# Four graph layers on one core: a kept order of the vector, scalar and GpSimd work of mixing and layer 1, some of it asked for a number of passes later

## Chip, cores and metric

The kernel runs on one core of a Trainium2 chip. The metric is the device time in microseconds (us) of one execution. The kernel before was run three times; their median is the number that the change is measured against. Besides, one execution was recorded by the profiler, and every duration in this text is from that one.

## What is computed

The input `x` has 8 batches of 2048 nodes with 64 features, and all four layers use the same 2048 x 2048 0/1 adjacency matrix. Each layer is a residual with a layer norm:

```
x = layernorm(x + L0(x, H, adj))   # hypergraph attention, mixed with adj/deg @ (x W_ind)
x = layernorm(x + L1(x, adj))      # dinv * (adj + I) * dinv @ x @ W^T
x = layernorm(x + L2(x, emb, adj)) # Chebyshev supports, softmax support, node-wise weights
x = layernorm(x + L3(x, adj))      # three rounds of relu(v W1v + adj v W1e) W2
```

Only the end of layer 0 and layer 1 matter here. In layer 0 two vectors of every node are mixed: `industry` (adj/deg @ x W_ind) and `g` (the attention). Each gets a score `tanh(f @ fcW + fcb) @ av`, a softmax over the two scores gives the weights, and the weighted sum is added to `x` and normalized. Layer 1 scales that by `dinv`, multiplies it with the adjacency, then with a 64 x 64 matrix, scales by `dinv` again, adds the residual and normalizes.

## The kernel before

**Tiling.** Two batches of 64 features fill 128 partitions, so the 8 batches are 4 *pairs* (p). The 2048 nodes are 4 *chunks* (c) of 512. `(p, c)` is one tile of 128 x 512 numbers, and there are 16 of them. The adjacency lies in SBUF the whole time. A product with it is split into a high and a low part (`split`, L165: `hi` is a rounded copy by ScalarE at L170, `lo` the rest by VectorE or GpSimd at L171), so one product of one pair is 2 halves (g) x 16 node tiles x 2 parts x 2 chunks = 128 matmuls of 128x512. One such matmul is called a *pass* in this text.

**The stage.** Mixing and layer 1 run interwoven. A Python generator, `filler`, gives out passes one at a time: first the rest of the products of layer 0 (`ug` in the profile), then `layer1(p)` for the four pairs (`u`). `fill(n)` asks for n passes. The loop over the *steps* i = 0..15 (one step is one tile of mixing) places the mixing's own TensorE work between them: `mix_scores(i)`, passes, `mix_end(i-1)`, passes, `mix_ind(i+1)` and `mix_g(i+1)`, passes, `mix_weigh(i)`, passes; 8 passes at each place, 9 from step 5 on. For one tile this is

- `mix_ind`: matmul `pi`, then VectorE `ind = pi * inv` (L823);
- `mix_g`: loads `gn` and `r` (a tile of x), four transposes `pg`, ScalarE `gt` (L838), GpSimd `r += gn` (L839);
- `mix_scores`: four matmuls `pf`, four ScalarE tanh (L851), two VectorE differences `t` (L853), GpSimd `ind -= gt` (L855);
- `mix_weigh`: matmuls `pd`, ScalarE `th` (L864), VectorE `ind *= th` (L865);
- `mix_end`: four transposes `pt`, VectorE `r += pt` (L873), then `layernorm`: VectorE mean (L142) and centring (L143), ScalarE square (L148), VectorE variance (L150, L152), GpSimd power (L154), VectorE scaling (L157), store of `r` to `x1_hbm` (L879).

`l1_parts` loads a stored tile back (`y`, L894), GpSimd scales it (L895), and `split` makes the two parts `v0h`..`v3l` that layer 1's passes read. At the end of each half of a pair ScalarE copies the two accumulators out (`ut`, L948); `l1_end` then runs on each: four matmuls `po`, a load of the residual `x1` (L903), VectorE `r = po * dinv` (L905), GpSimd `r += x1` (L906), and a layernorm without centring, whose result is stored to `x2_hbm` (L911).

**Buffers.** All small matmuls share four PSUM buffers (tag `mm`); `r` of the mixing, `gn`, `ut0`, `inv0`, the staged loads (`y`, `x1`, tag `x`) and `ut` have two buffers each, the parts `v0h`..`v3l` one each. So `r` of step i+1 is loaded into the buffer of step i-1, after the store of that one.

**What sets the order.** Each engine takes its instructions strictly in the order of its queue. The matmuls and transposes are kept in program order (`tc.keep_in_program_order`, L175 and L178). Nearly all other work of this stage is not: a scheduler in the framework places it in the queues of VectorE, ScalarE, GpSimd and SyncE (which issues the loads and stores) by its own estimate of when each would be ready. `later(n, f)` (L296) puts a piece of program off until n passes have gone by; `tick()` counts, once at each pass. Before, it is used for the last step of each layernorm (7 passes after the rest, through `put_off`) and for `l1_end` (6 and 14 passes after the half).

After the mixing, `mix_scope` closes, its memory becomes `xn`, the normalized x of all pairs. The embedding is loaded into parts of it (L1009), `load_xn` fetches the finished pairs back from `x2_hbm` on ScalarE's queue (L923), and `make_el` builds layer 2's factors (`pb`, `el`, `bias`) while the passes of the last pair run. Then come `s`, `pt` and `ua` of layer 2's softmax support.

Of the kernel before, what the change touches and what calls it, by code (L numbers as in the profile page):

```python
# [30 lines left out]
F32 = mybir.dt.float32  # L31
# [25 lines left out]
def tile_gnn_fast(  # L57
# [72 lines left out]
            s = slice(b * F, (b + 1) * F)  # L130
            nc.vector.tensor_scalar(t[s, s], t[s, s], mean[s], None, op0=ALU.subtract)

    def layernorm(pool, r, dst, groups=2 * JT, centred=False, small=None, tag="ln_c", bufs=1, put_off=None):


        xc = pool.tile([P, groups, F], F32, tag=tag, name="ln_c", bufs=bufs)
        pool = small or pool
        if centred:
            squares, xc = xc, r
        else:  # L140
            mean = pool.tile([P, groups], F32, tag="ln_m", name="ln_m", bufs=2)
            nc.vector.tensor_reduce(mean, r, AX.X, ALU.add)  # L142
            nc.vector.scalar_tensor_tensor(  # L143
                xc, mean[:, :, None].to_broadcast([P, groups, F]), -1.0 / F, r,
                op0=ALU.mult, op1=ALU.add,
            )
            squares = r
        nc.scalar.activation(squares, xc, AF.Square)  # L148
        var = pool.tile([P, groups], F32, tag="ln_v", name="ln_v", bufs=2)
        nc.vector.tensor_reduce(var, squares, AX.X, ALU.add)  # L150
        vare = pool.tile([P, groups], F32, tag="ln_e", name="ln_e", bufs=2)
        nc.vector.tensor_scalar(vare, var, 1.0 / F, EPS, op0=ALU.mult, op1=ALU.add)  # L152
        rstd = pool.tile([P, groups], F32, tag="ln_r", name="ln_r", bufs=2)
        nc.gpsimd.tensor_tensor(rstd, vare, neg_half[:, :groups], ALU.pow)  # L154

        def end():
            nc.vector.tensor_tensor(dst, xc, rstd[:, :, None].to_broadcast([P, groups, F]), ALU.mult)  # L157

        (put_off or (lambda f: f()))(end)

    def grouped(a):

        return a.rearrange("p t (b f) -> p (t b) f", f=F)
# [132 lines left out]
    def later(n, f):  # L296

        pending.append([n, f])

    def tick():  # L300
        for e in pending:
            e[0] -= 1
        while pending and pending[0][0] <= 0:
            pending.pop(0)[1]()

    places = {}
    xc, part = {}, {}
# [88 lines left out]
    def fill(n):  # L396
        for _ in range(n):
            if next(filler, None) == "wait":
                break

    def first_parts(c, where):
        where.add(c)
# [8 lines left out]
    with tc.tile_pool(name="pa_ps", bufs=1, space=PSUM) as pps:  # L411
# [42 lines left out]
        make_upper_triangular(nc, tri_e, 1.0, diag=True)  # L454


        def after(what):
            tc.keep_in_program_order(nc.gpsimd.tensor_copy(seen_x, what))

        for t in range(5):  # L460
            if t in (0, 2):
                after(xt[1 + t][:, 0, 0:1])
            load_adj(t, 0)
        tc.keep_in_program_order(nc.gpsimd.dma_start(flat[:, 0:MIX], mixing))

# [105 lines left out]
        for t in range(NT):  # L571
# [39 lines left out]
                    start=t == 0, stop=t == NT - 1,  # L611
                )
            if t in paced:
                after(seen[:, t, 0, 0:1])
                load_adj(paced[t], 0)
            if t in (9, 11):
                parts(0, (t - 9) // 2)
# [187 lines left out]

    uts, invs, gts, inds, tts, rs = {}, {}, {}, {}, {}, {}
    xn, done, stored, due = [], [0] * NP, set(), set()
    steps = NP * NCH

    def mix_load(i):  # L810
# [7 lines left out]
    def mix_ind(i):  # L818

        pi = lps.tile([P, C], F32, tag="mm", name="pi", bufs=4)  # L820
        mm(pi, lhsT=bd_ind, rhs=uts.pop(i), start=True, stop=True)
        inds[i] = mp.tile([P, C], F32, tag="ind", name="ind", bufs=3)
        nc.vector.tensor_tensor(inds[i], pi, invs.pop(i), ALU.mult)  # L823

    def mix_g(i):

        p, c = divmod(i, NCH)
        gn = mp.tile([P, JT, P], F32, tag="gn", name="gn", bufs=2)
        nc.sync.dma_start(
            gn, gs_hbm.rearrange("(p t) f -> p t f", t=NT)[:, wide(c), p * P:(p + 1) * P]  # L830
        )
        rs[i] = mp.tile([P, JT, P], F32, tag="r", name="r", bufs=2)
        load_x(rs[i], p, c)
        pg = lps.tile([P, C], F32, tag="mm", name="pg", bufs=4)
        for j in range(JT):
            transpose(pg[:, cols(j, P)], gn[:, j, :])
        gts[i] = mp.tile([P, C], F32, tag="gt", name="gt", bufs=2)
        nc.scalar.activation(gts[i], pg, AF.Identity, bias=-1.0)  # L838
        nc.gpsimd.tensor_tensor(rs[i], rs[i], gn, ALU.add)  # L839

    def mix_scores(i):

        t1 = []
        for src in (inds[i], gts[i]):
            for b in range(2):

                s = slice(b * F, (b + 1) * F)
                pf = lps.tile([P, C], F32, tag="mm", name="pf", bufs=4)
                mm(pf, lhsT=fc2[s, :], rhs=src[s, :], start=True, stop=True)
                t1.append(mp.tile([P, C], F32, tag="t1", name="t1", bufs=4))  # L850
                nc.scalar.activation(t1[-1], pf, AF.Tanh, bias=fcb_col)  # L851
        for b in range(2):
            nc.vector.tensor_tensor(t1[b], t1[b], t1[2 + b], ALU.subtract)  # L853
        tts[i] = t1[0:2]
        nc.gpsimd.tensor_tensor(inds[i], inds[i], gts[i], ALU.subtract)  # L855

    def mix_weigh(i):

        pd = lps.tile([P, C], F32, tag="mm", name="pd", bufs=4)
        for b in range(2):  # L860

            mm(pd[b * F:(b + 1) * F, :], lhsT=av2, rhs=tts[i][b], start=True, stop=True)
        th = mp.tile([P, C], F32, tag="th", name="th", bufs=1)
        nc.scalar.activation(th, pd, AF.Tanh, scale=0.5)  # L864
        nc.vector.scalar_tensor_tensor(inds[i], th, 1.0, inds[i], op0=ALU.add, op1=ALU.mult)  # L865

    def mix_end(i):
        p, c = divmod(i, NCH)
        r = rs.pop(i)
        pt = lps.tile([P, C], F32, tag="mm", name="pt", bufs=4)  # L870
        for j in range(JT):
            transpose(pt[:, cols(j, P)], inds[i][:, cols(j, P)])
        nc.vector.scalar_tensor_tensor(  # L873
            r, pt.rearrange("p (t f) -> p t f", f=P), 0.5, r, op0=ALU.mult, op1=ALU.add
        )

        def end(f):
            f()
            nc.sync.dma_start(x1_hbm[p][:, wide(c), :], r)  # L879
            stored.add((p, c))  # L880
            if p == 0:
                first_parts(c, mixed)
            elif (p, c) in due:
                l1_parts(p, c)

        layernorm(mp, grouped(r), grouped(r), put_off=lambda f: later(7, lambda: end(f)))

    def l1_parts(p, c):

        if (p, c) not in stored:  # L890
            due.add((p, c))
            return
        y = staged("y")
        nc.sync.dma_start(y, x1_hbm[p][:, wide(c), :])  # L894
        nc.gpsimd.tensor_tensor(y, y, dinv[:, wide(c), None].to_broadcast([P, JT, P]), ALU.mult)  # L895
        part[p, c] = split(va, y, f"v{c}", 1, [P, JT, P])

    def l1_end(p, c, ut):
        po = lps.tile([P, JT, P], F32, tag="mm", name="po", bufs=4)
        for j in range(JT):  # L900
            mm(po[:, j, :], lhsT=ut[:, cols(j, P)], rhs=bd_w1, start=True, stop=True)
        x1 = staged("x1")
        nc.sync.dma_start(x1, x1_hbm[p][:, wide(c), :])  # L903
        r = lp.tile([P, JT, P], F32, tag="r", name="r", bufs=2)
        nc.vector.tensor_tensor(r, po, dinv[:, wide(c), None].to_broadcast([P, JT, P]), ALU.mult)  # L905
        nc.gpsimd.tensor_tensor(r, r, x1, ALU.add)  # L906

        def end(f):
            f()
            if p < NP - 1:  # L910
                nc.sync.dma_start(x2_hbm[p][:, wide(c), :], r)  # L911
            done[p] += 1
            load_xn()

        dst = xn[p][:, wide(c), :] if p == NP - 1 else r
        layernorm(lp, grouped(r), grouped(dst), centred=True, put_off=lambda f: later(7, lambda: end(f)))

    def load_xn():

        for p in range(NP - 1):  # L920
            if xn and done[p] == NCH:
                done[p] = 0
                nc.scalar.dma_start(xn[p], x2_hbm[p][:])  # L923

    def layer1(p):

        for g in range(2):
# [17 lines left out]
                    l1_parts(p + 1, t // JT)  # L945
            for k, c in enumerate(own):
                ut = va.tile([P, C], F32, tag="ut", name="ut", bufs=2)
                nc.scalar.copy(ut, u[c])  # L948
                later(6 + 8 * k, lambda p=p, c=c, ut=ut: l1_end(p, c, ut))

    def all_pairs():
        yield from remaining
# [59 lines left out]

    ets = [load_emb(c, xn[NP - 1][:, wide(c), :].rearrange("p t f -> p (t f)")) for c in range(NCH)]

    load_xn()

    def make_el(c):
        et = ets[c]
# [13 lines left out]
    for c in range(NCH):  # L1032
        make_el(c)
        fill(16)
    norms = staged("emb").rearrange("p t f -> p (t f)")[:, 0:NT * D].rearrange("p (t d) -> p t d", d=D)
    nc.sync.dma_start(norms, emb.rearrange("(t p) d -> p t d", p=P))
    nc.vector.tensor_tensor(norms, norms, norms, ALU.mult)
# [14 lines left out]
    def apt_tile(c, t):  # L1052
# [4 lines left out]
        nc.scalar.activation(pt, s, AF.Exp)  # L1057
        nc.vector.tensor_scalar(pt, pt, 1.0, None, op0=ALU.max)  # L1058
        if t == 0:
            accs[c] = lp.tile([P, C], F32, tag="r", name="acc", bufs=2)  # L1060
            nc.gpsimd.tensor_copy(accs[c], pt)
        else:
            nc.gpsimd.tensor_tensor(accs[c], accs[c], pt, ALU.add)  # L1063
# [1125 lines left out]
```

## Time and profile before

| | |
|---|---|
| three runs | 1975.02, 1979.12, 1979.89 us, median 1979.12 |
| the profiled execution | 1976.23 us; its span from first to last instruction 1974.4 us |
| TensorE matmul busy | 1870.6 us, 95% of the span |
| VectorE, ScalarE, GpSimd busy | 1001.6, 394.6, 530.7 us |
| mean granted TensorE clock | 0.980 |
| mixing's first `pi` to last `pt` | 229.8 to 494 us |
| layer 1's first pass to last pass | 315.8 to 556.6 us |

How to read it: a profile row of the timeline has the start, the duration, the engine, the line of the kernel, the operation with what it writes and reads, its shape and count, and in brackets how long the engine had sat idle before and what ended that. PE is TensorE, DVE VectorE, ACT ScalarE, POOL GpSimd; `SPq` rows are DMAs that SyncE issues, and their duration is that of the issue. A busy matmul engine is not one at its peak: ends of matmuls are modelled and overlap, so the distance from start to start counts.

### The profile page before, as it was taken

The numbers are of one execution on the slowest core, as the hardware profiler recorded it, in microseconds if no ns is written. First come the engines' busy times: TensorE is split into PE (matmuls) and PEld (weight loads), VectorE is DVE, ScalarE is ACT, GpSimd is POOL, SyncE is SP. The second block draws the span as 40 slices with busy tenths as digits, with TensorE's granted clock in tenths as the row PEclk, the third lists the DMA queues.
The fourth block names the chain that finished last, engine by engine and source line by source line (L and its number), as shares of the span: only waits on it lengthen the run. The fifth ranks groups of instructions, "written<-read, shape, count | busy, mean of one in ns | idle before, by whom it ended". The sixth has DMA issues, their size and how long they took to land.

```text
span 1974.4 us, 19582 instructions
## 1 busy us (share of the span) xinstructions
PE 1870.6 (95%) x7100; PEld 1214.4 (62%) x7100; DVE 1001.6 (51%) x1741; ACT 394.6 (20%) x771; POOL 530.7 (27%) x480
## 2 busy tenths in 40 slices
PE   6888899888799999999999999999999999999997
PEld 4666566555554444755565575556546787877875
DVE  7779555556432211347546736764786333343332
ACT  1455343333121121100000000000001222222211
POOL 3678654544254344301001100110001020100101
PEclk9999899899899999999999999999999999999998
DMA  9923334332400000301101110111101122121211
GB/s 310 314 88 106 125 123 145 125 115 71 155 17 27 0 27 22 119 30 49 64 35 43 55 50 27 48 62 35 43 32 34 38 55 52 46 56 48 54 27 24
DMA packets 94185, 143.10 MB, mean 72 GB/s; under 512 B 29232, under 2 KB 40112, under 8 KB 93696
## 3 DMA queue, kind: packets, MB, share of 16 engines
q1 hardware_dynamic: 83920, 105.39, 17.2%
q0 software_dynamic: 7760, 27.66, 4.2%
q10 hardware_dynamic: 2400, 8.72, 1.2%
q8 instruction: 58, 0.95, 0.2%
q14 instruction: 47, 0.39, 0.1%
HBM read 98.67 MB, written 43.06 MB: 72 GB/s over the span
## 4 chain that ended last, share of the span: by engine, by line
PE 76%; DVE 4%; DMA 4%; POOL 4%; issue 3%; ACT 1%; SPq 1%; POOLq 0%; DVEq 0%; ACTq 0%
PE u L175 32%; PE py L175 22%; PE ua L175 11%; PE ug L175 3%; PE pr L175 2%; POOL ln_r L154 2%; PE po L175 1%; PE pf L175 1%; PE pt L178 1%; PE s L175 1%; DMA x<-x_hbm 1%; POOL r L906 1%; DMA r<-in_x_n 1%; DMA x_hbm<-r 1%; PE pd L175 0%
## 5 line engine op out<-in xcount | busy, mean ns | idle before, releaser
L175 PE MATMUL py<-wp,xg 128*128 128x512 f32 x1024 | 475.2, 592 | 0.7 <-DMA xg<-u_hbm 0.7
L175 PEld LDWEIGHTS py<-wp,xg 128*128 128x128 f32 x1024 | 193.3, 189 | 161.4 <-issue 138.5
L1276 DVE TENSOR_TENSOR fcav<-py,emb_n 128x512 f32<-128x512 f32 x256 | 177.0, 691 | 134.9 <-PE py L175 129.1
L175 PE MATMUL ua<-pt,xn 128*128 128x512 f32 x512 | 230.2, 592 | 1.5 <-DVE pt L1058 1.5
L154 POOL TENSOR_TENSOR ln_r<-ln_e,neg_half 128x8 f32<-128x8 f32 x64 | 108.1, 1688 | 458.0 <-DVE ln_e L152 425.0
L1277 DVE TENSOR_REDUCE r<-fcav 128x32 f32<-128x512 f32 x256 | 175.6, 686 | 8.2
L175 PEld LDWEIGHTS ua<-pt,xn 128*128 128x128 f32 x512 | 96.9, 190 | 110.9 <-issue 104.0
L175 PE MATMUL u<-adj,v0h 128*128 128x512 f32 x384 | 148.7, 455 | 1.3 <-ACT h L1432 1.3
L175 PE MATMUL u<-adj,v0l 128*128 128x512 f32 x384 | 141.3, 436 | 0.0
L175 PE MATMUL u<-adj,v2l 128*128 128x512 f32 x384 | 139.9, 429 | 1.2 <-DVE v2l L171 1.2
L175 PE MATMUL u<-adj,v2h 128*128 128x512 f32 x384 | 141.0, 433 | 0.0
L175 PE MATMUL u<-adj,v1h 128*128 128x512 f32 x384 | 140.7, 433 | 0.0
L175 PE MATMUL u<-adj,v3l 128*128 128x512 f32 x384 | 138.7, 426 | 0.0
L175 PE MATMUL u<-adj,v1l 128*128 128x512 f32 x384 | 138.4, 427 | 0.0
L175 PE MATMUL u<-adj,v3h 128*128 128x512 f32 x384 | 138.3, 427 | 0.0
L1063 POOL TENSOR_TENSOR acc<-acc,pt 128x512 f32<-128x512 f32 x60 | 76.8, 1280 | 103.9 <-DVE pt L1058 103.2
L1058 DVE TENSOR_SCALAR pt<-pt 128x512 f32<-128x512 f32 x64 | 30.2, 472 | 146.5 <-ACT pt L1057 146.2
L1358 DVE SCALAR_TENSOR_TENSOR ar<-fcav,ar 128x512 f32<-128x512 f32 x64 | 45.4, 709 | 109.1 <-ACT ar L1357 109.1
L175 PEld LDWEIGHTS u<-adj,v0h 128*128 128x128 f32 x384 | 71.6, 191 | 37.3 <-issue 24.5
L175 PEld LDWEIGHTS u<-adj,v2l 128*128 128x128 f32 x384 | 72.4, 190 | 32.2 <-issue 16.4
L175 PEld LDWEIGHTS u<-adj,v1l 128*128 128x128 f32 x384 | 72.8, 190 | 29.2 <-issue 14.4
L175 PEld LDWEIGHTS u<-adj,v3l 128*128 128x128 f32 x384 | 72.0, 188 | 29.4 <-issue 14.9
(354 smaller groups left out, 2669.5 us busy)
## 6 DMA issues: line engine op xcount, KB each, us to landing
adj<-in_adj_t POOLq DMA_DIRECT2D x32, 512.0 KB, 7.5
fcav<-in_adj_t SPq DMA_DIRECT2D x64, 256.0 KB, 2.9
u_hbm<-ut SPq DMA_DIRECT2D x48, 256.0 KB, 2.9
xg<-u_hbm SPq DMA_DIRECT2D x96, 128.0 KB, 2.9
x_hbm<-r SPq DMA_DIRECT2D x28, 256.0 KB, 2.1
hs_hbm<-st ACTq DMA_DIRECT2D x8, 584.0 KB
xt<-in_x_t SPq DMA_DIRECT2D x16, 256.0 KB, 6.6
ut<-u_hbm SPq DMA_DIRECT2D x16, 256.0 KB, 3.1
```

The lines of the kernel that those rows point to most:

```text
L154: nc.gpsimd.tensor_tensor(rstd, vare, neg_half[:, :groups], ALU.pow)
L175: tc.keep_in_program_order(nc.tensor.matmul(*args, **kw))
L178: tc.keep_in_program_order(nc.tensor.transpose(dst, src, ident))
L906: nc.gpsimd.tensor_tensor(r, r, x1, ALU.add)
L1058: nc.vector.tensor_scalar(pt, pt, 1.0, None, op0=ALU.max)
L1063: nc.gpsimd.tensor_tensor(accs[c], accs[c], pt, ALU.add)
L1276: nc.vector.tensor_tensor(pr, py, e_b, ALU.mult)
L1277: nc.vector.tensor_reduce(r[:, j, b, cols(k, OH)], pr, AX.X, ALU.add)
L1358: nc.vector.scalar_tensor_tensor(ar.bitcast(F32), seen_a, 1.0, ar.bitcast(F32), op0=ALU.mult, op1=ALU.not_equal, accum_out=left[:, t, k:k ...
```

## The change

The order of nearly all VectorE, ScalarE and GpSimd work of mixing and layer 1 is now kept as the program has it (`pin` is `tc.keep_in_program_order`). A new helper, `after(n, f, ...)`, asks for a piece n passes from now, and for the next one some passes after that one; unlike `later`'s list, in which a piece waits for those ahead of it, each entry runs when its own count is over. The layernorm of the two places becomes `normalized`, which gives three pieces: `square`, 5 passes later `power`, 9 passes later `scale`. `l1_load` makes the load of the residual a piece of its own, at the end of the half. `load_xn` works only once `room` is set, after the second `make_el`. The first accumulator of layer 2 lies in another tile. `fill` now counts a pass that can't be given yet, and goes on, where it stopped before. The old local `after` of the first stage is only renamed.

The instructions are the same in kind and number, and so is the order on TensorE, but for the four groups of `pb`, which come 9 passes later. On the other four queues the orders differ from the mixing's first steps (VectorE) or fifth step (the others) on, up to the first tiles of layer 2's softmax support, and are the same before and behind.

```diff
-    def layernorm(pool, r, dst, groups=2 * JT, centred=False, small=None, tag="ln_c", bufs=1, put_off=None):
+    def layernorm(pool, r, dst, groups=2 * JT, centred=False, small=None, tag="ln_c", bufs=1):
...
+    soon = []
+    def after(n, f, *more):
+        soon.append([n, lambda: (f(), after(*more) if more else None)])
     def tick():
-        for e in pending:
+        for e in pending + soon:
             e[0] -= 1
         while pending and pending[0][0] <= 0:
             pending.pop(0)[1]()
+        for e in [e for e in soon if e[0] <= 0]:
+            soon.remove(e)
+            e[1]()
...
+    def normalized(pool, r, dst, centred, then):
...
+        def square():
+            if not centred:
+                pin(nc.vector.tensor_reduce(mean, r, AX.X, ALU.add))
+                pin(nc.vector.scalar_tensor_tensor(
+                    xc, mean[:, :, None].to_broadcast(wide_r), -1.0 / F, r, op0=ALU.mult, op1=ALU.add
+                ))
+            pin(nc.scalar.activation(squares, src, AF.Square))
+        def power():
+            pin(nc.vector.tensor_reduce(var, squares, AX.X, ALU.add))
+            pin(nc.vector.tensor_scalar(vare, var, 1.0 / F, EPS, op0=ALU.mult, op1=ALU.add))
+            pin(nc.gpsimd.tensor_tensor(rstd, vare, neg_half[:, :groups], ALU.pow))
+        def scale():
+            pin(nc.vector.tensor_tensor(dst, src, rstd[:, :, None].to_broadcast(wide_r), ALU.mult))
+            then()
+        return square, 5, power, 9, scale
...
      def mix_ind(i):
-        nc.vector.tensor_tensor(inds[i], pi, invs.pop(i), ALU.mult)
+        inv = invs.pop(i)
+        after(3, lambda: pin(nc.vector.tensor_tensor(inds[i], pi, inv, ALU.mult)))
      def mix_g(i):
-        nc.gpsimd.tensor_tensor(rs[i], rs[i], gn, ALU.add)
+        r = rs[i]
+        after(8, lambda: pin(nc.gpsimd.tensor_tensor(r, r, gn, ALU.add)))
      def mix_scores(i):
+        def differences():
+            for b in range(2):
+                pin(nc.vector.tensor_tensor(t1[b], t1[b], t1[2 + b], ALU.subtract))
+        pin(nc.gpsimd.tensor_tensor(inds[i], inds[i], gts[i], ALU.subtract))
+        after(5, differences)
      def mix_weigh(i):
+        after(4, lambda: pin(
+            nc.vector.scalar_tensor_tensor(inds[i], th, 1.0, inds[i], op0=ALU.add, op1=ALU.mult)
+        ))
      def mix_end(i):
-        layernorm(mp, grouped(r), grouped(r), put_off=lambda f: later(7, lambda: end(f)))
+        after(3, add_up, 0, *normalized(mp, r, r, False, end))
      def l1_parts(p, c):
+        def scale():
+            pin(nc.gpsimd.tensor_tensor(y, y, dinv[:, wide(c), None].to_broadcast([P, JT, P]), ALU.mult))
+        def cast():
+            part[p, c] = split(va, y, f"v{c}", 1, [P, JT, P], pin=True)
+        after(16, scale, 6, cast)
 -    def l1_end(p, c, ut):
+    def l1_end(p, c, ut, x1):
-        layernorm(lp, grouped(r), grouped(dst), centred=True, put_off=lambda f: later(7, lambda: end(f)))
+        after(4, add_up, 6, *normalized(lp, r, dst, True, end))
      def layer1(p):
...
-                nc.scalar.copy(ut, u[c])
-                later(6 + 8 * k, lambda p=p, c=c, ut=ut: l1_end(p, c, ut))
+                pin(nc.scalar.copy(ut, u[c]))
+                later(6 + 8 * k, lambda p=p, c=c, ut=ut, x1=l1_load(p, c): l1_end(p, c, ut, x1))
...
     for c in range(NCH):
         make_el(c)
         fill(16)
+        if c == 1:
+            room.append(True)
+            load_xn()
```

More of the change, by code (lines that the diff above doesn't have):

```diff
@@ L154, in layernorm @@
         nc.gpsimd.tensor_tensor(rstd, vare, neg_half[:, :groups], ALU.pow)
-        def end():
-            nc.vector.tensor_tensor(dst, xc, rstd[:, :, None].to_broadcast([P, groups, F]), ALU.mult)
-        (put_off or (lambda f: f()))(end)
+        nc.vector.tensor_tensor(dst, xc, rstd[:, :, None].to_broadcast([P, groups, F]), ALU.mult)
     def grouped(a):
@@ L398, in fill @@
             if next(filler, None) == "wait":
-                break
+                tick()
     def first_parts(c, where):
@@ L454, in tile_gnn_fast, with behind @@
         make_upper_triangular(nc, tri_e, 1.0, diag=True)
-        def after(what):
+        def behind(what):
             tc.keep_in_program_order(nc.gpsimd.tensor_copy(seen_x, what))
@@ L461, in tile_gnn_fast @@
             if t in (0, 2):
-                after(xt[1 + t][:, 0, 0:1])
+                behind(xt[1 + t][:, 0, 0:1])
             load_adj(t, 0)
@@ L613, in tile_gnn_fast @@
             if t in paced:
-                after(seen[:, t, 0, 0:1])
+                behind(seen[:, t, 0, 0:1])
                 load_adj(paced[t], 0)
@@ L807, in tile_gnn_fast @@
     xn, done, stored, due = [], [0] * NP, set(), set()
+    pin = tc.keep_in_program_order
+    def normalized(pool, r, dst, centred, then):
+        groups = 2 * JT
+        r, dst = grouped(r), grouped(dst)
+        wide_r = [P, groups, F]
+        var, vare, rstd, mean = (
+            pool.tile([P, groups], F32, tag=f"ln_{n}", name=f"ln_{n}", bufs=2) for n in "verm"
+        )
+        xc = pool.tile(wide_r, F32, tag="ln_c", name="ln_c", bufs=1)
+        squares, src = (xc, r) if centred else (r, xc)
+        def square():
[13 more added lines that the diff above has]
+        return square, 5, power, 9, scale
     steps = NP * NCH
@@ L837, in mix_g @@
         gts[i] = mp.tile([P, C], F32, tag="gt", name="gt", bufs=2)
-        nc.scalar.activation(gts[i], pg, AF.Identity, bias=-1.0)
-        nc.gpsimd.tensor_tensor(rs[i], rs[i], gn, ALU.add)
+        pin(nc.scalar.activation(gts[i], pg, AF.Identity, bias=-1.0))
+        r = rs[i]
+        after(8, lambda: pin(nc.gpsimd.tensor_tensor(r, r, gn, ALU.add)))
     def mix_scores(i):
@@ L850, in mix_scores @@
                 t1.append(mp.tile([P, C], F32, tag="t1", name="t1", bufs=4))
-                nc.scalar.activation(t1[-1], pf, AF.Tanh, bias=fcb_col)
-        for b in range(2):
-            nc.vector.tensor_tensor(t1[b], t1[b], t1[2 + b], ALU.subtract)
+                pin(nc.scalar.activation(t1[-1], pf, AF.Tanh, bias=fcb_col))
         tts[i] = t1[0:2]
-        nc.gpsimd.tensor_tensor(inds[i], inds[i], gts[i], ALU.subtract)
+        def differences():
[3 more added lines that the diff above has]
+        after(5, differences)
     def mix_weigh(i):
@@ L863, in mix_weigh @@
         th = mp.tile([P, C], F32, tag="th", name="th", bufs=1)
-        nc.scalar.activation(th, pd, AF.Tanh, scale=0.5)
-        nc.vector.scalar_tensor_tensor(inds[i], th, 1.0, inds[i], op0=ALU.add, op1=ALU.mult)
+        pin(nc.scalar.activation(th, pd, AF.Tanh, scale=0.5))
+        after(4, lambda: pin(
+            nc.vector.scalar_tensor_tensor(inds[i], th, 1.0, inds[i], op0=ALU.add, op1=ALU.mult)
+        ))
     def mix_end(i):
@@ L872, in mix_end, with end @@
             transpose(pt[:, cols(j, P)], inds[i][:, cols(j, P)])
[L873 to L878, printed above, removed]
+        def end():
             nc.sync.dma_start(x1_hbm[p][:, wide(c), :], r)
@@ L884, in end, with add_up @@
                 l1_parts(p, c)
-        layernorm(mp, grouped(r), grouped(r), put_off=lambda f: later(7, lambda: end(f)))
+        def add_up():
+            pin(nc.vector.scalar_tensor_tensor(
+                r, pt.rearrange("p (t f) -> p t f", f=P), 0.5, r, op0=ALU.mult, op1=ALU.add
+            ))
+        after(3, add_up, 0, *normalized(mp, r, r, False, end))
     def l1_parts(p, c):
@@ L894, in l1_parts, with l1_load @@
         nc.sync.dma_start(y, x1_hbm[p][:, wide(c), :])
-        nc.gpsimd.tensor_tensor(y, y, dinv[:, wide(c), None].to_broadcast([P, JT, P]), ALU.mult)
-        part[p, c] = split(va, y, f"v{c}", 1, [P, JT, P])
-    def l1_end(p, c, ut):
+        def scale():
[3 more added lines that the diff above has]
+        after(16, scale, 6, cast)
+    def l1_load(p, c):
+        x1 = staged("x1")
+        nc.sync.dma_start(x1, x1_hbm[p][:, wide(c), :])
+        return x1
+    def l1_end(p, c, ut, x1):
         po = lps.tile([P, JT, P], F32, tag="mm", name="po", bufs=4)
@@ L901, in l1_end, with add_up, end @@
             mm(po[:, j, :], lhsT=ut[:, cols(j, P)], rhs=bd_w1, start=True, stop=True)
-        x1 = staged("x1")
-        nc.sync.dma_start(x1, x1_hbm[p][:, wide(c), :])
         r = lp.tile([P, JT, P], F32, tag="r", name="r", bufs=2)
[L905 to L909, printed above, removed]
+        def add_up():
+            pin(nc.vector.tensor_tensor(r, po, dinv[:, wide(c), None].to_broadcast([P, JT, P]), ALU.mult))
+            pin(nc.gpsimd.tensor_tensor(r, r, x1, ALU.add))
+        def end():
             if p < NP - 1:
@@ L915, in l1_end @@
         dst = xn[p][:, wide(c), :] if p == NP - 1 else r
-        layernorm(lp, grouped(r), grouped(dst), centred=True, put_off=lambda f: later(7, lambda: end(f)))
+        after(4, add_up, 6, *normalized(lp, r, dst, True, end))
+    room = []
     def load_xn():
         for p in range(NP - 1):
-            if xn and done[p] == NCH:
+            if room and done[p] == NCH:
                 done[p] = 0
@@ L1013, in tile_gnn_fast @@
     ets = [load_emb(c, xn[NP - 1][:, wide(c), :].rearrange("p t f -> p (t f)")) for c in range(NCH)]
-    load_xn()
     def make_el(c):
@@ L1059, in apt_tile @@
         if t == 0:
-            accs[c] = lp.tile([P, C], F32, tag="r", name="acc", bufs=2)
+            accs[c] = lp.tile([P, C], F32, tag="r", name="acc", bufs=2) if c else va.tile([P, C], F32, tag="v2h", name="acc", bufs=1)
             nc.gpsimd.tensor_copy(accs[c], pt)
```

## Prediction

> **What bounds the kernel now.** The page first. Its second part cuts the span into 40 slices of 49.4 us.
>
> ```profile
> PE   6888899888799999999999999999999999999997
> PEclk9999899899899999999999999999999999999998
> ```
>
> From the twelfth slice on (543 us) TensorE is full, and the change touches nothing there. Mixing and layer 1 are slices 5 to 11: 8, 9, 9, 8, 8, 8, 7 tenths, and where the busy share falls the granted clock falls too. So TensorE is the bound, and in this stage it is kept waiting. How much? The timeline of TensorE gives the measure of an unhindered step, from one `pf` to the next:
>
> ```profile
> 316.33 1.13 PE L175 MATMUL pf<-ind,fcav 64*128 64x512 f32 x4
> ...
> 329.79 1.13 PE L175 MATMUL pf<-ind,fcav 64*128 64x512 f32 x4
> ...
> 344.15 1.13 PE L175 MATMUL pf<-ind,fcav 64*128 64x512 f32 x4
> ```
>
> A step with its 36 passes takes 13.46 us, and 14.36 with one `po` of layer 1, which is thus 0.90. A pass is 0.233 (24 rows of two, 546.35 to 556.15, 0.467 each). From step 6's `pf` (316.33) to step 15's (474.93) are 9 steps with 9 `po`: 9 x 13.46 + 9 x 0.90 = 129.2. They took 158.6: **29.4 lost in the steps**. From there to the first `s` (556.62) are 186 passes (43.4), `pf` 1.9, two `pt` 0.9, `pd` 1.1, five `po` 4.5, four `pb` 4.5, together 56.3. They took 81.7: **25.4 lost in the tail**. The waits of TensorE between 225 and 560 us say on whom:
>
> ```profile
> PE po L175 <- ACT ut L948: 20.5, 4, 8.6
> PE pg L178 <- DMA gn<-gs_hbm: 5.1, 1, 5.1
> PE pt L178 <- DVE ind L865: 5.0, 1, 5.0
> PE pf L175 <- DVE ind L823: 4.3, 2, 3.9
> PE pb L175 <- DMA xn<-in_emb: 3.2, 1, 3.2
> PE pf L175 <- DVE r L905: 2.7, 1, 2.7
> ```
>
> (The second is at the stage's begin, before the change has moved anything that it waits for.) The longest, 8.6, read back through the timelines of the queues:
>
> ```profile
> 446.96 2.08 PE L175 MATMUL po<-bd_w,ut 128*128 128x128 f32 x8 [8.60 <-ACT ut L948]
> ...
> 445.23 0.62 ACT L170 CAST v3h<-y 128x512 fp32r<-128x512 f32 x1 [7.85 <-POOL y L895]
> 445.75 0.68 ACT L851 ACTIVATE t<-pf,fcav 128x512 f32<-128x512 f32 x1
> 446.33 1.06 ACT L948 COPY ut<-u 128x512 f32<-128x512 f32 x2
> ...
> 441.71 1.26 POOL L839 TENSOR_TENSOR r<-r,gn 128x512 f32<-128x512 f32 x1 [5.65 <-DMA r<-in_x_n]
> 442.93 1.26 POOL L855 TENSOR_TENSOR ind<-ind,gt 128x512 f32<-128x512 f32 x1
> 444.15 1.04 POOL L895 TENSOR_TENSOR y<-y,dinv 128x512 f32<-128x512 f32 x1
> ...
> 436.81 0.32 SPq L879 DMA_DIRECT2D x_hbm<-r  x1
> 439.00 0.33 SPq L290 DMA_DIRECT2D r<-in_x_n  x1
> ```
>
> Read from below: the store of `r` (2.19 until the load may be issued), the load (2.7 until GpSimd starts), and all the time GpSimd's queue stands with `r += gn` at its head. Behind it waits `y`; ScalarE's queue stands with the cast of `y` at its head, and the copy `ut`, whose passes ended long ago, waits behind that. No engine is full (in 330 to 500 us VectorE is busy 57%, GpSimd 48%, ScalarE 32%); it is queues with the wrong thing at their head.
>
> **The change part by part, TensorE's own work.** Unchanged in kind, number and order, except that the `pb` come 9 passes later. Cost 0.
>
> **The kept order in the steps.** Laid out in time after a step's `pf`, with these rows' durations and no layer-1 work: tanh ends at 2.9, the differences (asked after 5 passes) end 4.4, `pt` 4.0 to 4.4, `r += pt`, mean, centring until 6.5, square 7.2, variance 8.2, power 9.9, scaling 10.7, store 12.9, load 15.6, `r += gn` 16.9, which is 3.4 in the next step. There `r` is needed at 4.4 of the step after it, and `gn`, freed by it, a step later too. No wait of TensorE comes from that. So what hides the cost is that nobody needs GpSimd from 9.9 to 15.6.
>
> With layer 1 there is somebody. `r += gn` is asked for 17 passes after `pt`, one pass *ahead* of the scaling, store and load that it needs. GpSimd is then held for scaling 0.69, store 2.2, load 2.7, 5.6 us in each step, and behind it stand `ind -= gt`, `r += x1`, both powers and the scaling of `y`. Its work per step is 1.27 + 1.29 + 1.65 for the mixing, and 9/8 of a layer-1 tile, 1.125 x (1.29 + 1.65 + 1.04) = 4.5: 8.7, with the hold 14.3, against a step of 13.46 + 1.125 x 0.90 = 14.5. It just fits, with no slack, so it doesn't set the pace but delays whatever falls into the hold. I followed the four queues of the changed kernel step by step with these durations:
>
> - Step 8 (two `po`): `r += x1` ends at 4.8 and 7.4, both powers by 13.3, every PSUM buffer is free in time: 0.
> - Step 9: the load of `r` stands on SyncE's queue behind the load of `y`, which waits for VectorE until 0.6; `r += gn` ends 5.2, `ind -= gt` 6.5, two `y` 8.7. ScalarE casts the first `y` at 7.7 and VectorE, kept in order, does `r += pt` only at 9.1. Centring ends 11.1, square 11.8, `gt`, then `ut` at 12.9. TensorE wants `po` at 9.2: wait 3.7.
> - Step 10: the square of a layer-1 tile stands ahead of the four tanh and waits for `r += x1` until 3.2: `pt` waits 0.5, and `ind` is ready at 15.4 instead of 13.5: 1.9.
> - Step 12, the same with the second tile's square: 0.7 and 1.4. Step 13: the cast of `y` holds ScalarE to 10.8 and VectorE to 11.5, so a `po` gives its PSUM buffer back at 12.1 and `pg` waits 3.1. Steps 14 and 15: about 1 each.
>
> Together 13.3 of waiting, where the steps have 19.6 now (3.93, 2.35, 2.70, 1.59, 0.38, 8.60).
>
> A wait costs more than itself: 29.4 lost for 19.6 waited. The Trainium skill (TensorE: Matmul & The Clock Gate, Part 1) says that the clock halves after an idle window of some 3.4 us and comes back after as long a busy one. By that rule only step 9's wait pays, half of 3.4: 13.3 + 1.7 = 15.0. But here the `po` after a wait of only 2.35 took 1.65 instead of 1.05. I take the row: 0.5 more for each us of the four longest (3.7, 3.1, 2.4 and 2.1, each step's taken together), 5.6, so 18.9 is left. **Gain in the steps 29.4 - 18.9 = 10.5.**
>
> A second rule speaks against the change: the skill (SBUF — State Buffer, two separate sides) says that a VectorE instruction with two SBUF inputs and a GpSimd one that reads SBUF lock each other out for a whole instruction. The rows: a scaling right behind the power, with GpSimd going on, takes 1.52 to 1.76 (at 360.33, 365.48, 385.86), alone 0.69 (436.09); differences at 352.47 still take 0.64 each. VectorE's work per step is 9.5 (mixing 6.2, layer 1 1.125 x 2.9). By the rows, with 2.1 scalings at 0.9 more, 11.4 of 14.5: hidden. By the rule, with some 6.5 such instructions, 15.4: VectorE the bound, 0.9 x 10 steps = 9 us more. I take the rows, and keep 9 for the range.
>
> **The tail.** `pd` and `pt` of step 15 wait 1.59 and 4.95 for VectorE, whose queue has a scaling at its head that waits for a power. In the kept order the weighing stands ahead of that scaling, but behind two variances: 2 left. `pb` waits 3.16 for the embedding, which waits for the last `r` to be stored. The chain from step 15's `pt` is 15.6 (493.16 to 508.75), TensorE's 50 passes and two `po` are 13.5: 2 left. The `po` that waits 7.49 goes free: `ut` now stands ahead of the last two casts of `y`, not behind. (The last `y` took 10.3 to load, beside two loads of 1 MB for `xn`; now one of these is issued there. With a load of some 8 it reaches its cast 22 us after `pt`, when the passes need it: 1.5 left as the price of that cover.) The `po` that waits 2.11 for a store of `bias` goes free, since those loads are spread. Left 5.5 of 19.3, in time lost 6: **gain 25.4 - 6 = 19.5.** The passes come back to layer 2 with nothing else late: its first `ua` keeps its 1.48.
>
> **Sum.** 10.5 + 19.5 = 30. 1976.2 - 30 = 1946.2 for an execution like the profiled one, which lies 2.9 under the median of the runs: 1949.
>
> **Bounds of what isn't shown.** The new layout can't give more than all of the loss, 54.8, that is 1924. From the other side each hold may be worth a 3.7 wait as in step 9: ten steps, 37 x 1.5 = 55 lost in the steps.
>
> **The rivals.** (a) *The loss nearly goes away.* My layout takes each queue strictly and adds delays up; if the holds fall where nothing waits, as in step 8, both parts keep some 5: gain 45, 1934. For it: no engine is over 66% of a step. Against: the hold of 5.6 on GpSimd is in each step. (b) *One part only.* The tail gains, the steps don't (new holds for old), 1979 - 19.5 = 1960; or the embedding and `y` keep the tail's loss and only the steps gain, 1969. (c) *No change*, within 0.3%: the tail's gain is paid back in the steps. (d) *Slower: GpSimd's queue becomes the bound.* It has 14.3 of 14.5 us already. If besides the hold it waits for VectorE ahead of `r += x1` and of a power, 2.4 and 2.1 as the rows show now, a step takes 18.8: 4.3 over, ten steps 43, with the clock's half more 65 lost instead of 29.4. Less the tail's 19.5, 16 slower: 1995. It decides from 0.2 us of waiting per step on; for it speaks that a kept order can't step over a late one. Against: these waits mostly lie within the hold.
>
> **Chances.** Forecast 1949 (1939 to 1957) 0.55; (a) 0.15; (b) 0.17; (c) 0.06; (d) 0.07. Within 0.3% (6 us) is about what a measurement of this kernel can't tell from no change. Faster 0.87, same 0.06, slower 0.07. The range 1931 to 1970 leaves out (c), (d) and the far end of (a).
>
> **What would show it.** Right: TensorE's waits for `po` fall from 20.5 to under 6; GpSimd idle 4 to 6 us before each `r += gn`, ended by the load; a step's `pf` to `pf` at 13.5 to 14.4 where no wait is left; the first `s` near 527. Wrong: the wait for `ind` (L862) ahead of `pf` grows over 4 us in several steps (rival d); or a `u` pass waits for `v3h` or `v3l` in the tail.

## The result, and the profile after it

| | before | after |
|---|---|---|
| median of the runs on one chip | 1978.28 us (4 runs, 1975.02 to 1979.89) | 1965.34 us (4 runs, 1964.57 to 1967.83) |
| ratio to before, 95% interval | | 0.9939 [0.9922, 0.9956] |
| span of the profiled execution | 1974.4 | 1963.5 |
| step 6's `pf`, step 15's `pf`, first `s` | 316.33, 474.93, 556.62 | 317.91, 482.39, 544.80 |
| lost in the steps (their length less 129.2) | 29.4 | 35.3 |
| lost in the tail (its length less 56.3) | 25.4 | 6.1 |

The kernel is faster, by 13 us instead of the 30 that were forecast. The tail did what was forecast. The steps, which were to gain 10.5, lost 5.9 more than before. With 1.6 lost ahead of step 6 and 0.9 behind the first `s`, this is the whole difference of the two spans: 19.3 - 5.9 - 1.6 - 0.9 = 10.9.

The page's second part of the changed kernel, with the same two rows as before:

```profile
PE   6889899888999999999999999999999999999997
PEclk9999899989999999999999999999999999999998
```

Slice 11, which holds most of the tail, is now at 9 tenths (7 before); slices 8 to 10 (mostly the steps with layer 1) still stand at 8. The same in exact windows. First the kernel before, then the changed one; a row has the window, its length, then busy us (with the number of instructions) of TensorE, its weight loads, VectorE, ScalarE and GpSimd, then the granted clock, the DMA share and GB/s. The first row of each is the steps, the second the tail.

```profile
316.30:474.90 158.60, 139.05 (x595) 90.99 (x594) 90.04 (x133) 52.76 (x91) 75.06 (x54) 0.94 0.35 113
474.90:556.60 81.70, 62.41 (x279) 47.88 (x279) 40.84 (x71) 17.43 (x32) 30.25 (x21) 0.90 0.34 115
```

```profile
317.90:482.40 164.50, 142.54 (x595) 92.34 (x596) 93.38 (x134) 52.95 (x93) 77.06 (x58) 0.92 0.35 112
482.40:544.80 62.40, 58.52 (x280) 44.71 (x279) 39.34 (x71) 16.54 (x31) 28.87 (x20) 1.00 0.48 154
```

The work in the windows is nearly the same before and after; the tail now runs at full clock, the steps at less than before. Whom TensorE waits for in the stage says the same (line, releaser, sum, number, longest):

```profile
PE po L171 <- ACT ut L1007: 10.0, 3, 7.2
PE pd L171 <- DVE t L896: 4.7, 2, 2.4
PE pf L171 <- DVE ind L862: 3.8, 4, 3.1
PE pt L174 <- ACT t L891: 3.6, 2, 3.4
```

`po` waits half as long as before, but `pd` and `pt` now wait for the scores of the mixing, which did not appear in the steps of before. In the steps the waits are 2.24 (`pd` of step 6), 7.19 (`po` of step 9), 3.09 (`pf` of step 11), 3.38 (`pt` of step 12), 0.86, 1.91 (`pg` of step 13), 2.42 (`pd` of step 14) and four of about 0.2: 22.0 together, where before had 19.6 and the forecast 13.3. The longest, read through the queues of the changed kernel:

```profile
365.00 1.13 PE L171 MATMUL pf<-ind,fcav 64*128 64x512 f32 x4 [0.25 <-DVE ind L862]
382.11 2.08 PE L171 MATMUL po<-bd_w,ut 128*128 128x128 f32 x8 [7.19 <-ACT ut L1007]
...
376.87 0.62 ACT L166 CAST v1h<-y 128x512 fp32r<-128x512 f32 x1 [6.56 <-POOL y L944]
380.47 0.63 ACT L834 ACTIVATE r<-ln_c 128x512 f32<-128x512 f32 x1 [2.98 <-DVE ln_c L831]
381.00 0.58 ACT L877 ACTIVATE gt<-pg 128x512 f32<-128x512 f32 x1
381.48 1.06 ACT L1007 COPY ut<-u 128x512 f32<-128x512 f32 x2
...
377.52 0.86 DVE L167 TENSOR_TENSOR v1l<-y,v1h 128x512 fp32r<-128x512 f32 x1 [6.46 <-ACT v1h L166]
378.31 0.68 DVE L929 SCALAR_TENSOR_TENSOR r<-pt,r 128x512 f32<-128x512 f32 x1
...
373.33 1.29 POOL L879 TENSOR_TENSOR r<-r,gn 128x512 f32<-128x512 f32 x1 [5.99 <-DMA r<-in_x_n]
374.58 1.27 POOL L898 TENSOR_TENSOR ind<-ind,gt 128x512 f32<-128x512 f32 x1
...
365.57 0.32 SPq L921 DMA_DIRECT2D x_hbm<-r  x1
368.74 0.32 SPq L941 DMA_DIRECT2D y<-x_hbm  x1
369.16 0.41 SPq L286 DMA_DIRECT2D r<-in_x_n  x1
```

This is the old chain in a new place: `r` is stored, the same buffer is loaded again, GpSimd stands 5.99 us with `r += gn` at its head, behind it `y`, and behind that ScalarE's cast. Here the new order adds a piece: VectorE does `v1l` ahead of `r += pt`, so the centring comes late, and on ScalarE the square that waits for it (2.98) and `gt` stand ahead of `ut`, for which TensorE waits. The reorganized queues kept the one request that made the old chain.

### The profile page after: what moved, and what is told of

It reads as the page before. It is cut to its first block, busy times and chain, and to the rows that moved or that the text cites. A ratio compares the mean times of both kernels' runs of the same rounds, so it can differ in the third digit from the quotient of the medians.

```text
span 1963.5 us, 19567 instructions
## 1 busy us (share of the span) xinstructions
PE 1872.4 (95%) x7100; PEld 1213.1 (62%) x7100; DVE 1005.2 (51%) x1741; ACT 392.7 (20%) x771; POOL 528.3 (27%) x480
## 4 chain that ended last, share of the span: by engine, by line
PE 74%; DMA 5%; POOL 3%; DVE 3%; issue 2%; ACT 1%; SPq 0%; POOLq 0%; ACTq 0%; DVEq 0%
PE u L171 32%; PE py L171 22%; PE ua L171 11%; PE pr L171 2%; PE ug L171 2%; DMA r<-in_x_n 1%; DMA x_hbm<-r 1%; POOL ln_r L839 1%; PE po L171 1%; PE pf L171 1%; PE s L171 1%; PE pt L174 1%; DVE r L842 1%; PE pn L174 0%; POOL y L944 0%
## 5 line engine op out<-in xcount | busy, mean ns | idle before, releaser
L154 POOL TENSOR_TENSOR ln_r<-ln_e,neg_half 128x8 f32<-128x8 f32 x32 | 53.5, 1671 | 399.0 <-DVE ln_e L152 369.6
L171 PEld LDWEIGHTS u<-adj,v1l 128*128 128x128 f32 x384 | 72.7, 190 | 29.1 <-issue 14.4
```

The costliest lines, as they stand in the source:

```text
L171: tc.keep_in_program_order(nc.tensor.matmul(*args, **kw))
```

## The experiments

The theory (A in what was expected): the kept order is good, but `r += gn` is asked for too early, and in a kept order GpSimd's queue must then stand at each step until the buffer of `r` has been stored and loaded. Then asking later for it, or a third buffer, must give back the steps. Whether that needs the kept order too was left open. Rivals: the kept order itself costs the steps (VectorE and GpSimd in each other's way, or an engine made to wait out of turn), or the steps' loss is one of transfers. Each ratio is to runs of the kernel before on the same chip (medians 1978.28 to 1981.99). "Lost in steps / tail" is worked out as in the table above, from the one profiled execution of each; executions of one kernel differ by 3 to 14 us, and those profiled of e3_free and e5_before_three_r lay 4 us under their medians, so a few us between two splits say nothing. Medians of runs on different chips are compared below too; by the ratios these differences come out up to 4 us larger or smaller.

| run | median us | ratio to before [95%] | lost in steps / tail |
|---|---|---|---|
| changed kernel | 1965.34 | 0.9939 [0.9922, 0.9956] | 35.3 / 6.1 |
| e1_late_add | 1938.97 | 0.9789 [0.9764, 0.9813] | 2.3 / 8.3 |
| e2_three_r | 1939.08 | 0.9791 [0.9768, 0.9814] | 7.5 / 5.1 |
| e3_free | 1974.22 | 0.9972 [0.9963, 0.9980] | 26.9 / 18.0 |
| e4_xn_early | 1973.12 | 0.9968 [0.9957, 0.9980] | 32.4 / 15.9 |
| e5_before_three_r | 1973.56 | 0.9969 [0.9960, 0.9980] | 24.6 / 23.6 |
| e6_free_late | 1973.61 | 0.9974 [0.9965, 0.9983] | 28.2 / 18.8 |
| e7_add_20 | 1947.65 | 0.9837 [0.9819, 0.9855] | 11.9 / 10.2 |
| e8_late_cast | 1956.68 | 0.9890 [0.9873, 0.9908] | 17.7 / 14.0 |
| e9_late_three_r | 1942.45 | 0.9795 [0.9778, 0.9812] | 4.6 / 9.9 |
| e10_scalar_free | 1947.86 | 0.9832 [0.9816, 0.9849] | 6.8 / 11.3 |
| e11_scalar_only | 1958.74 | 0.9890 [0.9874, 0.9907] | 19.8 / 13.4 |
| e12_kept_at_once | 2008.62 | 1.0146 [1.0129, 1.0163] | 52.5 / 28.3 |

**Ask for `r += gn` later.** In the changed kernel:

```diff
-        after(8, lambda: pin(nc.gpsimd.tensor_tensor(r, r, gn, ALU.add)))
+        after(34, lambda: pin(nc.gpsimd.tensor_tensor(r, r, gn, ALU.add)))
```

> The changed kernel with one number changed: GpSimd's r += gn is asked for 34 passes after mix_g, not 8. Theory A (the hold): in the changed kernel r += gn stands at the head of GpSimd's queue for 5.8 us in each of 11 steps, ahead of work that is ready, and that makes most of the 35 us lost in the steps. Then the holds before r += gn fall from 63 us to under 10, the steps lose 15 to 20 us, and the time is about 1948 us. Theory B (casts and squares): the casts of y and the squares of layer 1, kept ahead of tanh, gt and ut on ScalarE, hold it whatever GpSimd does, and the hold on GpSimd is hidden: 1960 to 1967 us.

One number moved 26 passes gives 26.4 us, more than theory A had expected (1948): the steps lose 2.3, not 15 to 20. How long GpSimd stood ahead of `r += gn` between 300 and 500 us, first in the changed kernel, then here (sum, number):

```profile
  POOL r L879: 63.5, 11
```

```profile
  POOL r L879: 15.0, 5
```

63.5 is 5.8 in each of 11 steps; 15.0 is left, in five. Step 9 of this run:

```profile
362.70 1.13 PE L171 MATMUL pf<-ind,fcav 64*128 64x512 f32 x4
...
378.21 1.13 PE L171 MATMUL pf<-ind,fcav 64*128 64x512 f32 x4
...
371.57 1.06 ACT L1007 COPY ut<-u 128x512 f32<-128x512 f32 x2
...
368.70 1.28 POOL L879 TENSOR_TENSOR r<-r,gn 128x512 f32<-128x512 f32 x1 [1.99 <-DMA r<-in_x_n]
```

`ut` is copied 8.9 us after `pf` (16.5 in the changed kernel), and the two `po` of this step wait for nothing: 15.51 from `pf` to `pf`, of which 13.46 and twice 0.90 are due. The steps' clock:

```profile
320.50:452.00 131.50, 129.81 (x595) 86.07 (x594) 97.54 (x134) 53.50 (x93) 77.49 (x57) 1.00 0.42 138
```

The clock is back at 1.00 and TensorE is busy 129.8 of 131.5 us. VectorE has more busy time than in the changed kernel (97.5 against 93.4) and costs nothing, so it was not the bound. Nor were the transfers: about the same bytes went through in less time (138 GB/s over 131.5 us against 112 over 164.5).

**A third buffer instead.** The request stays where the change put it; `r` need not wait for the store:

```diff
-        rs[i] = mp.tile([P, JT, P], F32, tag="r", name="r", bufs=2)
+        rs[i] = mp.tile([P, JT, P], F32, tag="r", name="r", bufs=3)
```

> The changed kernel with three buffers for the mixing's r instead of two, so that the load of r doesn't wait for the store two steps back; the order on GpSimd stays as it is (r += gn asked for 8 passes after mix_g). Theory A (the hold of GpSimd by store and load of r): the load is long there, the hold goes, about 1948 us, the same as with the later request. Theory B (casts and squares hold ScalarE anyway): 1960 to 1967 us.

The same time by another way. No `r += gn` waits for its load any more. So it is the standing of GpSimd's queue that cost the steps, and not the order of the requests in itself; the granted clock is back at 0.99 with it, so the lower clock was a consequence. VectorE is busy 102.4 of 136.7 us here, still hidden.

**Both.** The third buffer in e1_late_add.

> The changed kernel with both the late request (34) and the third buffer of r. If the late request has taken out all of the hold, the third buffer adds nothing: 1937 to 1941 us. If the load of gn, which follows r on SyncE's queue, or the rest of the holds before r += gn (15 us in five steps) still cost: 2 to 4 us less, 1935 us.

1942.45 against 1938.97 (ratios 0.9795 and 0.9789, the intervals overlap): the second cure adds nothing to the first, as it should if both do the same thing.

**About half as late.** `after(20` in place of `after(34`.

> The changed kernel with r += gn asked for 20 passes after mix_g, between the 8 of the change and the 34 of the late request. The load is there about 33 passes after mix_g, so some 3 of the 5.8 us of hold in each step stay. If the loss follows the hold in proportion: about 1952 us. If a hold costs only where it is longer than the slack of what stands behind it (about half of it): nearer to the late request, 1940 to 1945 us.

Between the two: 17.7 under the changed kernel, 8.7 above e1_late_add, and between the two figures expected. The loss in the steps follows the request (35.3, 11.9, 2.3 for 8, 20, 34 passes).

**The order let go.** The changed kernel with all its later requests, but with nothing pinned save the matmuls and transposes (the scheduler orders, as before); and the same with the late `r += gn`:

```diff
-    pin = tc.keep_in_program_order
+    pin = lambda i: i
...
-            part[p, c] = split(va, y, f"v{c}", 1, [P, JT, P], pin=True)
+            part[p, c] = split(va, y, f"v{c}", 1, [P, JT, P])
```

> The changed kernel without the kept order: the scheduler places all work of VectorE, ScalarE and GpSimd again, the later requests stay. Theory A: the scheduler places r += gn by its own estimate of the load, as before, so the steps lose about what they lost before (29 us), the tail keeps the gain: about 1960 us. Theory B: casts and squares that wait can be placed behind tanh and ut: the steps lose 20 us or less, about 1950 us. If the tail's gain came from the kept order (ut ahead of the casts), it goes, and the time is 1975 or more.

> The changed kernel with r += gn asked for 34 passes after mix_g, and without the kept order: the scheduler places everything again. If the late request is all that is needed, as long as the load has come: 1945 to 1950 us (the steps near 5 lost, the tail as in the free order, 18). If a kept order is needed besides: 1960 us or more.

And the kernel before with the third buffer for `r`:

> The kernel before, with three buffers for the mixing's r and nothing else. If the hold of GpSimd by store and load of r is the cause of the steps' loss there too (29 us), and order and requests don't matter, the steps' loss goes: about 1955 us, with the tail's 25 left. If the scheduler's order of casts, squares and adds is what loses, the buffer changes little: 1975 to 1980 us.

The four corners: not kept, 1974.22 (request at 8) and 1973.61 (at 34); kept, 1965.34 and 1938.97. Without the kept order the late request is worth nothing, and the third buffer alone is worth 0.3% (e5_before_three_r); with it each is worth 26 us. The order alone is worth 9 with the hold, 35 without. So the change needs both halves, and had one. Theory A missed e3_free: it had 1960, with the steps as before and the tail's gain kept; the steps lost 26.9, but most of the tail's gain went as well.

**The kept order without later requests.** The changed kernel with three buffers for `r` and `after` made to run all its pieces at once, at the place of the first:

```diff
-        soon.append([n, lambda: (f(), after(*more) if more else None)])
+        f()
+        if more:
+            after(*more)
```

> The kept order without the later requests: each piece is asked for at once, where it stood before the change; three buffers for r, so that the hold of r is not in play (with the later requests and three buffers: 1939 us). If the kept order alone makes the gain: 1945 us or less. If the later requests are needed, each scaling, difference and cast stands at the head of its queue until its input is there: 1985 us or more, slower than before.

1.5% slower than before, and 69.5 us slower than e2_three_r, from which only the requests differ. VectorE's queue in front of a `pf` that waits 8.53 us for `ind`, at 373.66:

```profile
368.62 0.69 DVE L839 TENSOR_REDUCE ln_v<-r 128x8 f32<-128x512 f32 x1 [0.69 <-ACT r L836]
369.34 0.17 DVE L840 TENSOR_SCALAR ln_e<-ln_v 128x8 f32<-128x8 f32 x1
371.26 1.74 DVE L844 TENSOR_TENSOR r<-ln_c,ln_r 128x512 f32<-128x512 f32 x1 [1.75 <-POOL ln_r L841]
372.92 0.68 DVE L864 TENSOR_TENSOR ind<-pi,inv 128x512 f32<-128x512 f32 x1
```

`ind = pi * inv` needs nothing of the layernorm, but stands behind all of it, with the waits for ScalarE's square and GpSimd's power (0.69 and 1.75) in between. This is what a kept order is without the spacing. (The scaling is asked for at once here too; the kernel before put it off by 7 passes. So the comparison with before is not of the order alone.)

**Which engines' order.** e1_late_add with ScalarE's work let go, the pins on VectorE and GpSimd staying; and the reverse, pins on ScalarE alone.

> The changed kernel with the late request (34), the kept order on VectorE and GpSimd only; ScalarE's order in the stage is the scheduler's. If ScalarE's order (casts and squares ahead of ut) is what the free order loses by: 1965 us or more. If it is the order on GpSimd and VectorE: 1937 to 1945 us.

> The counterpart: the late request (34), the kept order on ScalarE only, VectorE and GpSimd in the scheduler's order. If ScalarE's order is what the free order loses by: 1937 to 1945 us. If it is that of GpSimd and VectorE: 1965 us or more. If both are needed, this one and its counterpart both lie over 1955.

8.9 and 19.8 us above e1_late_add: ScalarE's order is worth something, VectorE's and GpSimd's together more. Neither run came out as one part alone would have it (1937 to 1945), and e10_scalar_free did not reach the 1955 that was set for "both are needed". VectorE and GpSimd were not taken apart; with ScalarE's alone TensorE waits 6.9 us for `ind *= th` and 3.7 for `ind`, both VectorE's.

**The casts later.** In e1_late_add, `after(16, scale, 6, cast)` becomes `after(16, scale, 16, cast)`.

> The late request (34) with the casts of y asked for 32 passes after their load instead of 22; the passes need them after 48. With the late request alone one wait over 2 us was left, a po of the tail for 3.4, whose ut stands on ScalarE behind a cast that waits for y. If the cast then comes behind ut: 3 to 5 us less than the late request, about 1935 us. If a later cast makes a pass wait for its part, as much is lost again: 1939 to 1943 us.

A miss of the idea that the casts have room: 17.7 us lost, outside both figures expected. TensorE's waits in this run:

```profile
PE u L171 <- ACT v3h L166: 6.4, 2, 3.6
```

The passes themselves wait for their operand. A request can be too late as well, here by ten passes (2.3 us of TensorE's time).

**The tail: the loads of `xn` where they were.** In the changed kernel `room` is set and `load_xn()` called ahead of `make_el`, as before.

> The changed kernel with the loads of xn allowed as soon as the mixing's memory is free, as before the change. The tail gained 19 us. If the moved loads make it (the last y and x1 load without them beside): the tail loses 8 or more of it again, 1973 us or more. If the kept order of ut ahead of the last casts makes it, and the loads are hidden: 1965 to 1968 us.

7.8 us slower, 9.8 of loss in the tail. ScalarE's queue and the `po`, in this run:

```profile
505.85 0.81 ACTq L982 DMA_DIRECT2D xn<-x_hbm  x2
506.70 0.62 ACT L166 CAST v1h<-y 128x512 fp32r<-128x512 f32 x1 [8.15 <-issue]
507.23 1.07 ACT L1007 COPY ut<-u 128x512 f32<-128x512 f32 x2
...
507.86 2.08 PE L171 MATMUL po<-bd_w,ut 128*128 128x128 f32 x8 [5.78 <-ACT ut L1007]
```

The two loads are issued on ScalarE's queue, into memory of the mixing that comes free with the store of its last `r` (issued at 503.37); until then they stand ahead of a cast and of `ut`, and TensorE waits 5.78 where it waited 1.90. In the tail 9.8 of the 19.3 go when those loads go back, so about half comes from moving them. The rest goes with the kept order: with the loads moved and nothing pinned (e3_free) the tail loses 18.0, with `po` waiting 4.93 and 4.00. The later `pb` and the moved accumulator were not tried apart.

## Why the prediction was right and wrong

**The tail: right, size too.** Forecast 19.5 of gain and 6 left; measured 19.3 and 6.1. The waits forecast as 2 for `pb` and 2 for `pd` and `pt` were 1.07 and 0.91; no pass waited for the last cast (1.5 was forecast), and one `po` waited 1.90 for `ut`, which was not forecast; so the total agrees better than its parts, which is in part luck. The load of the last `y` was to fall from 10.3 to some 8 with one load of `xn` moved away, and it did: it landed 7.9 after its issue (9.9 in e4_xn_early). What the forecast did not see is that moving those loads also frees ScalarE's queue, as e4_xn_early shows.

**The steps: wrong.** The failed step is the layout that left 13.3 us of waiting in the steps, and with it 18.9 lost. There were 22.0, and 35.3 lost. The path was seen rightly: the hold of GpSimd, then `y`, the cast, `ut`. Its sentence on GpSimd, "It just fits, with no slack, so it doesn't set the pace but delays whatever falls into the hold", had the load right: 8.6 of work a step (77.06 in 9) and a hold of 5.8, against 8.7 and 5.6. What it made of it was wrong. A queue without slack can't make up a delay and hands it to the next step; the layout let each hold begin on time. Step 9 shows it. By the layout `r += gn` ends 5.2 after `pf`; it ended 9.6 after. The load of `r` was issued at 4.2 instead of 5.2 - 1.3 - 2.7 = 1.2: it stands on SyncE's queue behind the load of `y`, and that waited for the end of VectorE's `v0l`, 3.7 after `pf` and not 0.6.

```profile
368.02 0.69 DVE L167 TENSOR_TENSOR v0l<-y,v0h 128x512 fp32r<-128x512 f32 x1
```

It then took 4.2 until GpSimd's start instead of 2.7, issued right behind the load of `y`. From there on all is late by as much: `po` starts at 17.1 instead of 12.9 and waits 7.19 instead of 3.7. Of the 8.7 us of waiting beyond the layout, 3.5 are this wait, 2.2 the one of step 6, for which the layout had nothing, and most of the rest lies where it had a wait, but a shorter one (step 10 and the `pf` behind it 3.3 for 2.4, step 12 3.4 for 2.1). A slip in the forecast is without effect: the stretch from 546.35 to 556.15 has 22 rows of two passes, not 24, and its 0.467 each holds.

Where the first 3.0 came from is read in the rows of step 8, where the forecast let VectorE's differences take 0.64 each:

```profile
353.40 3.51 DVE L896 TENSOR_TENSOR t<-t,t 128x512 f32<-128x512 f32 x2 [3.24 <-ACT t L891]
358.14 1.18 DVE L838 TENSOR_SCALAR ln_e<-ln_v 128x8 f32<-128x8 f32 x1
...
353.40 1.27 POOL L879 TENSOR_TENSOR r<-r,gn 128x512 f32<-128x512 f32 x1 [5.65 <-DMA r<-in_x_n]
354.63 1.73 POOL L964 TENSOR_TENSOR r<-r,x 128x512 f32<-128x512 f32 x1
...
358.04 1.26 POOL L964 TENSOR_TENSOR r<-r,x 128x512 f32<-128x512 f32 x1
```

The held GpSimd instruction and VectorE's two start at the same moment, and these took 2.2 more than alone; the tensor_scalar at 358.14 took 1.18 instead of 0.17. The times fit two engines that take turns by whole instructions: `r += gn` until 354.67, one difference, `r += x1` until 356.36, the other difference until 356.91; and the tensor_scalar ends with GpSimd's second `r += x1`, at 359.3. Not all of this delays the chain, since the variance behind the differences needs a square that ended at 357.03. An estimate from these rows: without the turns `r += pt`, which started at 359.24, could have started at 357.4, so 1.8 of the 3.0 is this. Another 1.0 was there already: step 8's `r += gn` ended 4.4 after its `pf`, where the layout had 3.4.

So the rule of the Trainium skill on the locked port (SBUF — State Buffer, two separate sides), which the forecast set aside for the rows, does bear on this (as the forecast put it, not on the tensor_scalar, which has one such input). One row that it was set aside for was misread: the differences at 352.47 took 0.64 each because nothing ran beside them, GpSimd being idle from 352.00 to 354.43. But the lock acts not by making an engine the bound (VectorE was busy 10.4 of 18.3 us a step, and 11.4 of 15.2 in e2_three_r, the fast one), but as a delay in a chain that has no slack. That this delay began step 9's is argued from the rows; no run takes it away by itself.

**The clock.** The price of the waits beyond themselves was 9.8 for 19.6 waited before and 13.3 for 22.0 after. The granted clock of the steps, 0.94 and 0.92, gives the same: 158.6 x 0.06 = 9.5 and 164.5 x 0.08 = 13.2. The forecast took 0.5 for each us of the four longest only, 5.6. Of the 16.4 that the steps' loss was off, 8.7 is more waiting and 7.7 is this price. By the rule of the skill (TensorE: Matmul & The Clock Gate, Part 1), only the 7.19 and, just about, the 3.38 reach its window, half of 3.4 each: 22.0 + 3.4 = 25.4. By the forecast's row, taken on all waits, 33. The measured 35.3 is nearer the row, but the price is not one for each us. Read in stretches of 1 us, the changed kernel's clock stood at 0.50 for some 3.4 us behind the waits of 1.91, 2.24, 2.42 and 3.38 (1.7 lost each), longer behind the 3.09 (2.9 lost), and 1.5 were lost behind the 7.19: 11.3 of the 13.3. So here waits well under 3.4 halved the clock, for about as long as the rule says it takes to come back. Not each did: in e4_xn_early it stayed at 1.00 behind waits of 2.18 and 2.69. And two runs with the same 8.2 us of waiting in the steps paid 3.7 (e7_add_20, one wait over 1.6) and 9.5 (e8_late_cast, three) beyond them.

**The rivals.** It is (b), one part only, with its "new holds for old"; (b) had a chance of 0.17, and this form of it stood at 1960. It came out 5 later, since the new holds cost 5.9 more than the old. Of (d) the mechanism was there, GpSimd at 14.4 of a step; a step took 18.3, where (d) said 18.8. But 43 of that case's 65 was GpSimd's own pace, and the sum of TensorE's waits was 22: it waits in seven places, not in each step. (a) at 1934 is what e1_late_add and e2_three_r nearly reach (1939), once the hold is gone: the kept order was worth about that much. (c) did not happen.

**The signs named.** `po` under 6: no, 10.0. GpSimd idle 4 to 6 ahead of each `r += gn`: yes, 5.8 on average. First `s` near 527: no, 544.80; with the hold removed, 516.65. `pf` to `pf` at 13.5 to 14.4 where no wait is left: yes in step 7, 14.36. `pf` waiting over 4 for `ind` in several steps: no, 3.09 at most. A `u` pass waiting for `v3h` or `v3l` in the tail: no.

## What to carry to other kernels

Where a queue's order is kept by hand, each instruction must be asked for only when its slowest input will be there: count the whole way of that input (here scaling, store, load into the same buffer), and place the request behind it, or give it another buffer. An order that is kept but asked for at once is worse than the scheduler's (2008.62 against 1979), and one request in the wrong place took 26 of the 40 us that the order was worth. A queue whose work and holds just fill a step is not "just fitting": it can't make up a delay, so each delay of another engine goes on to the next step.

## What was not expected of the hardware

VectorE's two-input instructions and GpSimd's held each other up more when the kernel was fast, not less: VectorE's busy time in the steps was 90.0 before, 93.4 after, 97.5 in e1_late_add and 102.4 in e2_three_r, for nearly the same instructions, while the time fell. The mixing's scaling took 1.75 at the median in the steps of e2_three_r, in the changed kernel 0.69. DMA issues that stand in ScalarE's queue held it 8.15 us in e4_xn_early, which the profile puts down to issue and not to a wait.
